# TensorE's instruction order written by the program in a 32-head attention and feed-forward kernel

## The chip, the cores and the metric

The kernel runs on one core of a Trainium2 chip. The time is the device time of one execution in microseconds (us); the figure for a kernel is the median of three runs. A profile is one further execution taken by the hardware profiler; its span runs from the first to the last instruction.

## The reference

The input is 1,024 tokens of 512 numbers, in float32. Attention has 32 heads with 128 numbers for each query, key and value, and is causal. It is followed by a three-layer feed-forward net whose weights are +1 or -1.

```python
x = x + attn(layernorm(x), wq, wkv, wo)
x = x + ffn(layernorm(x), k0, s0, k1, s1, k2, s2)

# attn
q = x @ wq;  k, v = split(x @ wkv)                 # 32 heads of 128
scores = where(causal, q @ k.T * 192 ** -0.5, -1e30)
attn = softmax(scores) @ v
return attn.reshape(S, 32 * 128) @ wo

# ffn
h = relu(s0 * (x @ sign(k0))) * 2
h = relu(s1 * (scaled(h) @ sign(k1))) * 2
return s2 * (scaled(h) @ sign(k2))
```

## The kernel before

**Stages.** The tokens are normalised and transposed into `xnT` (features on the partitions, 1,024 tokens in a row). Queries and keys of the first two heads are computed plainly (`qk_plain`, L256). Then a loop of 256 steps, one for each head and block of 128 queries (L590), does all of attention. The feed-forward net comes last (L724 on).

**Pairs of heads.** Heads go in pairs `g`, 16 steps to a pair; `s` is the step in the pair and `qt` the query block in the head. In the steps of pair `g` TensorE has five kinds of work:

- the scores of the next step's query block, `probabilities` (L448), against all keys up to it, so the work grows with `qt`. The scores have one buffer of two PSUM banks (`ps_sc`, bufs 1), so those of the next step wait until VectorE has read these ones (L458, which also forms `nmax`);
- the products for the pair's values and for the next pair's queries and keys (`products`, L268). Each projection is done by seven half-size products in place of eight (a Strassen-like scheme, with sums of the weights on GpSimd and the combinations on VectorE and ScalarE): 21 products in a pair, in the order values, queries, keys;
- the attention of a head's first 512 queries (the **early attend**, `qb` 0: 4 key blocks) and of its last 512 (the **late attend**, `qb` 1: 8 key blocks), `attend` (L552);
- the products with `wo` for the pair before, 14 parts (`o_products`, L397), which VectorE adds up in `acc`.

**Softmax.** For each step: VectorE adds the mask and finds the row's extreme (L458), ScalarE does the exponential (L469), VectorE the reciprocal (L473), ScalarE the scaling (L474), and VectorE transposes the result in blocks of 32x32 into `tb[qb]` (L480).

**The exchange.** These blocks must still change partitions. `exchange` (L515) does it with DMAs on the SP queue (L524), 16 to a **piece** of four key blocks. A head has three pieces: one for its early attend, two for its late attend. The pieces come from the tile pool `pairs` under the tag `pT`, which has two buffers (L68, L520); a piece can be filled only when the attend that read the buffer before is done with it. `exchange(h, 0)` is written at the step with `qt` 3 and `exchange(h, 1)` at `qt` 7. In the kernel before, the matching `attend` is written four steps later (L620): the early attend at `qt` 7 of its own head, the late one at `qt` 3 of the next.

**What sets the order.** Each engine works through its own instruction stream in order. That stream is made by the tile framework when the program is built: it gives the instructions a priority by their place in the program and puts the first that is ready, by its own model of the times, next on the engine. So an instruction may be put ahead of, or behind, the place where it is written, and one `attend` may be cut in two. The SP queue carries the exchanges and all loads of weights: queries and keys (L122), values (L128) and `wo` (L132).

**The last head** is done differently: its steps run in the order `qt` 4 to 7, 0 to 3, its probabilities are transposed on TensorE (`transpose_last`, L508), and the sums of the `wo` products (`add_products`) and the direct products for the last pair (`o_unit`, L434) fall between its steps.

Of the kernel before, what the change touches and what calls it, by code (L numbers as in the profile page):

```python
# [13 lines left out]
P = 128  # L14
# [15 lines left out]
def kernel(  # L30
# [27 lines left out]
    wq_v = wq.rearrange("(c p) (h e) -> p c h e", p=P, e=DQ)  # L58
    wkv_v = wkv.rearrange("(c p) e -> p c e", p=P)
    wo_v = wo.rearrange("(h p) d -> p h d", p=P)  # L60

    def pool(name, bufs, **kw):
        return ctx.enter_context(tc.tile_pool(name=name, bufs=bufs, **kw))
# [189 lines left out]
        )  # L253
        return dst[h]

    def qk_plain(which, h):  # L256
        dst = new_qk(which, h)
        w = w_raw[which, h // G][:, h % G]
        for half in range(NQB):
            cols = slice(half * QB, (half + 1) * QB)  # L260
            ps = ps_mm.tile([P, QB], F32, tag="mm", name=f"ps_{'qk'[which]}{h}_{half}")
            for c in range(NC):
                nc.tensor.matmul(
                    ps, lhsT=w[:, c, :], rhs=xnT[:, c, cols], start=(c == 0), stop=(c == NC - 1)
                )
            nc.scalar.activation(dst[:, cols], ps, AF.Copy, scale=(-scale, 1.0)[which])

    def products(which, g):  # L268


        s = w_sum[which, g]
        mul = (-scale, 1.0, 1.0)[which]
        n = f"{'qkv'[which]}{g}"
        if which == 2:
            d = []
            for h in (g * G, g * G + 1):
                vs[h] = heads.tile([P, NT, DV], F32, tag="v", name=f"v{h}", bufs=3)
                d.append([vs[h][:, k * TPB : (k + 1) * TPB, :] for k in range(NQB)])
        else:
            d = [  # L280
                [t[:, k * QB : (k + 1) * QB] for k in range(NQB)]
                for t in (new_qk(which, g * G), new_qk(which, g * G + 1))
            ]

        def bank(name):
            shape = [P, TPB, DV] if which == 2 else [P, QB]
            return ps_st.tile(shape, F32, tag="st", name=f"{name}_{n}")

        def kept(name):
            shape = [P, TPB, DV] if which == 2 else [P, QB]  # L290
            return const.tile(shape, F32, tag=name, name=f"{name}_{n}")

        def product(ps, a, b, first, last):
            for c in range(2):
                start, stop = first and c == 0, last and c == 1
                if which != 2:
                    nc.tensor.matmul(  # L297
                        ps,
                        lhsT=a[:, c, :],
                        rhs=b[:, c, :],  # L300
                        start=start,
                        stop=stop,
                        skip_group_check=True,
                    )
                    continue
                for t in range(TPB):
                    nc.tensor.matmul(  # L307
                        ps[:, t, :],
                        lhsT=b[:, c, t * P : (t + 1) * P],
                        rhs=a[:, c, :],  # L310
                        start=start and t == 0,
                        stop=stop and t == TPB - 1,
                        skip_group_check=True,
                    )

        def plus(out, ps, other):
            if which == 0:
                nc.vector.scalar_tensor_tensor(out, ps, mul, other, ALU.mult, ALU.add)
            else:
                nc.vector.tensor_tensor(out, ps, other, ALU.add)  # L320

        X = bank("X")
        product(X, A(which, g, 0, 0), B(0, 0), True, False)
        p1 = kept("p1")
        nc.scalar.activation(p1, X, AF.Copy, scale=mul)  # L325
        yield
        Y = bank("Y")
        product(Y, s[1], T[1], True, False)
        u2 = kept("u2")
        plus(u2, Y, p1)  # L330
        yield
        product(X, A(which, g, 0, 1), B(1, 0), False, True)
        nc.scalar.activation(d[0][0], X, AF.Copy, scale=mul)
        yield
        product(Y, s[2], T[2], False, False)
        u3 = kept("u3")
        plus(u3, Y, p1)
        yield
        Z = bank("Z")
        product(Z, s[0], T[0], True, False)  # L340
        plus(d[1][1], Z, u3)
        yield
        product(Y, A(which, g, 1, 1), T[3], False, True)
        plus(d[1][0], Y, p1)
        yield
        product(Z, s[3], B(1, 1), False, True)
        plus(d[0][1], Z, u2)
        yield
# [25 lines left out]
    def o_products(g):  # L374


        def a(d, i):
            return wo_sb[g][:, i, d * DH : (d + 1) * DH]

        if g not in o_sum:  # L380
            o_sum[g] = sums_of(a, "osum", f"osum{g}", 1)
        s = o_sum[g]
        for m, left, right in (
            (0, lambda: attn[g * G, 0], a(0, 0)),
            (1, lambda: attn[g * G + 1, 0], a(0, 1)),
            (3, lambda: a_sum[g][0], s[0]),
            (2, lambda: a_sum[g][2], s[2]),
            (4, lambda: a_sum[g][1], s[1]),
            (5, lambda: a_sum[g][3], a(1, 1)),
            (6, lambda: attn[g * G + 1, 1], s[3]),  # L390
        ):
            left = left()
            for half in range(2):
                ps = ps_mm.tile([P, 2, DH], F32, tag="mm", name=f"ps_o{g}_{m}_{half}")
                for i in range(2):
                    tok = slice((2 * half + i) * P, (2 * half + i + 1) * P)
                    nc.tensor.matmul(  # L397
                        ps[:, i, :], lhsT=left[:, tok], rhs=right, start=True, stop=True
                    )
                dst = acc[:, m, 2 * half : 2 * half + 2, :]  # L400
                if g == 0:
                    nc.vector.tensor_copy(dst, ps)
                else:
                    nc.vector.tensor_tensor(dst, dst, ps, ALU.add)  # L404
                yield
# [24 lines left out]
    def o_unit(g, t):  # L430
        ps = ps_mm.tile([P, D], F32, tag="mm", name=f"ps_o{g}_{t}")
        k, i = divmod(t, TPB)
        for j in range(G):
            nc.tensor.matmul(  # L434
                ps,
                lhsT=attn[g * G + j, k][:, i * P : (i + 1) * P],
                rhs=wo_sb[g][:, j, :],
                start=(j == 0),
                stop=(j == G - 1),
            )  # L440
        nc.vector.tensor_tensor(xs[t], xs[t], ps, ALU.add)

    def probabilities(h, qt):
        n = (qt + 1) * P
        sc = ps_sc.tile([P, S], F32, tag="sc", name=f"sc{h}_{qt}")
        for first in range(0, n, QB):
            cols = slice(first, min(first + QB, n))
            nc.tensor.matmul(  # L448
                sc[:, cols],
                lhsT=qT[h][:, qt * P : (qt + 1) * P],  # L450
                rhs=kT[h][:, cols],
                start=True,
                stop=True,
            )
# [76 lines left out]
    def attend(h, qb, pieces):  # L531
# [4 lines left out]
        if h == H - 1:  # L536
            ps = ps_mm.tile([P, TPB, P], F32, tag="mm", name=f"ps_av{h}_{qb}")
            for kc in range(nk):
                first = max(0, kc - qb * TPB)
                nc.tensor.matmul(  # L540
                    ps[:, first:, :],
                    lhsT=vs[h][:, kc, :],
                    rhs=last_pT[qb][kc // 2][:, kc % 2, first:, :],
# [5 lines left out]
        ps = ps_mm.tile([P, NB, TPB, B32], F32, tag="mm", name=f"ps_av{h}_{qb}")  # L549
        for kc in range(nk):  # L550
            first = max(0, kc - qb * TPB)
            nc.tensor.matmul(  # L552
                ps[:, :, first:, :],
                lhsT=vs[h][:, kc, :],
                rhs=pieces[kc // TPB][:, kc % TPB, :, first:, :],
                start=(kc == 0),
                stop=(kc == nk - 1),
            )
# [1 line left out]
        if qb == 1 and g + 1 < NG:  # L560
            attn_sums(g, early=(j == 0))

    for which in range(2):
        for h in range(G):
            qk_plain(which, h)
    token_sums()
    weight_sums(2, 0)

# [13 lines left out]
    def softmax_step(h, qt):  # L582
# [3 lines left out]
        else:  # L586
            transpose_last(qt, p)

    softmax_step(*steps[0])
    for i, (h, qt) in enumerate(steps):  # L590
        g, j = divmod(h, G)
        s = i % (G * NT)
        if s == 0:
            chain = products_of_pair(g)
            if g + 1 < NG:
# [17 lines left out]
                load_qk_weights(0, g + 2)  # L613
        if i + 1 < len(steps):
            softmax_step(*steps[i + 1])
        for _ in range(1 + s % 2):
            next(chain, None)
        if qt % TPB == TPB - 1 and h < H - 1:
            qb = qt // TPB
            to_attend[i + TPB] = (h, qb, exchange(h, qb))  # L620
        if i in to_attend:
            attend(*to_attend.pop(i))
        if g > 0 and s >= 2:
            next(o_chain, None)
            if g == NG - 1 and s < 8:
                next(o_chain, None)
        if h == H - 1:
            if qt == 5:
                add_products(x_out)
            if qt == 0:  # L630
                attend(h, 1, None)
# [57 lines left out]
    def hidden_layer(i, k, src, dst):  # L689
        hi, lo = dst  # L690
        for oc in range(NC):
            ps = ffn_bank(f"ps_h{i}_{k}_{oc}")
            for c in range(NC):
                for part in range(2):
                    nc.tensor.matmul(  # L695
                        ps,
                        lhsT=w_sign[i][c][:, oc * P : (oc + 1) * P],
                        rhs=src[part][:, c, :],
# [8 lines left out]
    def output_layer(k):  # L707
        for t in range(k * TPB, (k + 1) * TPB):
            ps = ffn_bank(f"ps_out{t}")
            cols = slice((t % TPB) * P, (t % TPB + 1) * P)  # L710
            for c in range(NC):
                for part in range(2):
                    nc.tensor.matmul(
                        ps,
                        lhsT=h2[k][part][:, c, cols],
                        rhs=w_sign[2][c],
# [60 lines left out]
```

## Time and profile before

| | |
|---|---|
| median of three runs | 1395.57 us (1394.65 to 1396.83) |
| the profiled execution's time | 1395.0 us |
| its span | 1393.2 us |
| TensorE busy | 1358.0 us |
| VectorE busy | 790.8 us |
| ScalarE busy | 491.2 us |
| GpSimd busy | 283.6 us |
| mean granted TensorE clock | 0.997 |

The span is 1.8 us shorter than the execution's time; the rest lies around it. On TensorE a float32 matrix product of one instruction in the program stands as two records in the trace (scores of 512 keys and 128 queries are two records of 128x512). The records' own durations overlap, because matmuls are pipelined; what one costs is read from the distance between starts. "PE" is TensorE's matmul, "DVE" is VectorE, "ACT" ScalarE, "POOL" GpSimd, and "SPq" the queue that issues the DMAs. A row of the waits gives the total, the number and the longest of one kind of wait.

### The profile page before, as it was taken

The numbers are of one execution on the slowest core, as the hardware profiler recorded it, in microseconds if no ns is written. First come the engines' busy times: TensorE is split into PE (matmuls) and PEld (weight loads), VectorE is DVE, ScalarE is ACT, GpSimd is POOL, SyncE is SP. The second block draws the span as 40 slices with busy tenths as digits, with TensorE's granted clock in tenths as the row PEclk, the third lists the DMA queues.
The fourth block names the chain that finished last, engine by engine and source line by source line (L and its number), as shares of the span: only waits on it lengthen the run. The fifth ranks groups of instructions, "written<-read, shape, count | busy, mean of one in ns | idle before, by whom it ended". The sixth has DMA issues, their size and how long they took to land.

```text
span 1393.2 us, 16661 instructions
## 1 busy us (share of the span) xinstructions
PE 1358.0 (97%) x5396; PEld 858.1 (62%) x5396; DVE 790.8 (57%) x1656; ACT 491.2 (35%) x921; POOL 283.6 (20%) x337
## 2 busy tenths in 40 slices
PE   7999999999999999999999999999999999998798
PEld 4647575656657575665757566575756657575467
DVE  3454665555565655556665645565555556656575
ACT  3444343332433333334333323433332343233322
POOL 5211112131111213112121311212131121202400
PEclk9999999999999999999999999999999999999999
DMA  4234434344343434434343443434344343425301
GB/s 151 60 97 104 105 82 123 86 120 104 94 113 83 122 85 125 101 93 119 81 126 83 127 101 91 126 75 127 84 126 102 93 123 77 126 68 143 94 1 61
DMA packets 266421, 139.31 MB, mean 100 GB/s; under 512 B 26208, under 2 KB 259168, under 8 KB 266336
## 3 DMA queue, kind: packets, MB, share of 16 engines
q1 hardware_dynamic: 266336, 138.25, 38.8%
q8 instruction: 44, 0.72, 0.2%
q14 instruction: 41, 0.34, 0.1%
HBM read 38.54 MB, written 2.10 MB: 29 GB/s over the span
## 4 chain that ended last, share of the span: by engine, by line
PE 87%; SPq 5%; DVE 5%; DMA 2%; issue 1%; ACT 0%; POOL 0%; DVEq 0%; ACTq 0%
PE sc L448 16%; PE ps_av L552 15%; PE ps_o L397 11%; PE Y_v L307 6%; PE Y_k L297 5%; PE Y_q L297 5%; SPq L524 5%; PE X_v L307 4%; PE Z_v L307 4%; PE Z_k L297 4%; PE X_q L297 3%; PE X_k L297 3%; PE Z_q L297 3%; PE ps_h L695 2%; DVE tb L480 2%; DMA pT<-tb 1%
## 5 line engine op out<-in xcount | busy, mean ns | idle before, releaser
L469 ACT ACTIVATE p<-p,nmax 128x128 f32<-128x128 f32 (+7 forms) x256 | 197.5, 772 | 396.6 <-DVE nmax L458 395.0
L448 PE MATMUL sc<-kT,qT 128*128 128x512 f32 (+3 forms) x768 | 298.5, 497 | 14.8 <-DVE nmax L458 14.3
L552 PE MATMUL ps_av<-pT,v 128*128 128x512 f32 x744 | 255.4, 486 | 0.0
L458 DVE CUSTOM_DVE_ANT_0 p<-sc,mask 128x128 f32<-128x128 f32 (+7 forms) x256 | 191.3, 747 | 94.1 <-PE sc L448 92.1
L474 ACT ACTIVATE p<-p,rtotal 128x128 f32<-128x128 f32 (+7 forms) x256 | 195.0, 771 | 88.8 <-DVE rtotal L473 88.3
L448 PEld LDWEIGHTS sc<-kT,qT 128*128 128x128 f32 x768 | 136.6, 191 | 142.3 <-issue 82.7
L404 DVE TENSOR_TENSOR acc<-acc,ps_o 128x512 f32<-128x512 f32 x196 | 131.9, 681 | 160.1 <-PE ps_o L397 159.0
L552 PEld LDWEIGHTS ps_av<-pT,v 128*128 128x128 f32 x744 | 140.0, 190 | 129.3 <-issue 107.6
L480 DVE STREAM_TRANSPOSE tb<-p 128x128 f32<-128x128 f32 (+1 forms) x248 | 178.4, 756 | 17.8 <-ACT p L474 14.5
L397 PE MATMUL ps_o<-wo,attn 128*128 128x256 f32 x360 | 87.7, 383 | 0.6 <-POOL attn L369 0.6
L473 DVE RECIPROCAL rtotal<-total 128x1 f32<-128x1 f32 x256 | 39.6, 155 | 74.7 <-ACT p L469 74.3
L397 PEld LDWEIGHTS ps_o<-wo,attn 128*128 128x128 f32 x360 | 67.2, 190 | 20.4 <-issue 8.1
L236 POOL TENSOR_TENSOR wsumq<-wq 128x256 f32<-128x256 f32 x15 | 10.9, 725 | 332.8 <-DMA wq<-in_L_attn_wq_dram 243.7
L307 PEld LDWEIGHTS X_v<-wv,xnT 128*128 128x128 f32 x512 | 63.3, 192 | 4.2 <-issue 0.5
L307 PE MATMUL X_v<-wv,xnT 128*128 128x128 f32 x512 | 65.1, 275 | 0.0
L559 DVE COPY attn<-ps_av 128x512 f32<-128x512 f32 x62 | 41.9, 676 | 37.9 <-PE ps_av L552 37.9
L397 PE MATMUL ps_o<-osum,at 128*128 128x256 f32 x240 | 61.4, 379 | 0.0
L297 PE MATMUL X_q<-xnT,wq 128*128 128x512 f32 x120 | 57.2, 592 | 0.0
L297 PE MATMUL X_k<-xnT,wk 128*128 128x512 f32 x120 | 57.1, 593 | 0.0
L236 POOL TENSOR_TENSOR wsumk<-wk 128x256 f32<-128x256 f32 x15 | 10.9, 725 | 223.7 <-DMA wk<-in_L_attn_wkv_dram 207.3
L397 PEld LDWEIGHTS ps_o<-osum,at 128*128 128x128 f32 x240 | 44.4, 190 | 17.8 <-issue 12.6
L325 ACT ACTIVATE p_k<-X_k 128x512 f32<-128x512 f32 x15 | 8.9, 591 | 114.9 <-PE X_k L297 101.5
(162 smaller groups left out, 1736.0 us busy)
## 6 DMA issues: line engine op xcount, KB each, us to landing
pT<-tb SPq DMA_DIRECT2D x1488, 64.0 KB, 2.0
wq<-in_L_attn_wq_dram SPq DMA_DIRECT2D x32, 256.0 KB, 3.3
wk<-in_L_attn_wkv_dram SPq DMA_DIRECT2D x32, 256.0 KB, 3.4
wv<-in_L_attn_wkv_dram SPq DMA_DIRECT2D x16, 512.0 KB, 4.3
wo<-in_L_attn_wo_dram SPq DMA_DIRECT2D x16, 512.0 KB, 5.0
x_in<-_attn_hidden_states_dram SPq DMA_DIRECT2D x8, 256.0 KB, 5.1
x_out<-_attn_hidden_states_dram SPq DMA_DIRECT2D x8, 256.0 KB, 4.8
out_dram<-osb SPq DMA_DIRECT2D x8, 256.0 KB, 2.0
```

What stands on the lines that cost most here:

```text
L297: nc.tensor.matmul(ps, lhsT=a[:, c, :], rhs=b[:, c, :], start=start, stop=stop, skip_group_check=True,)
L307: nc.tensor.matmul(ps[:, t, :], lhsT=b[:, c, t * P : (t + 1) * P], rhs=a[:, c, :], start=start and t == 0, stop=stop and t == TPB - 1, ski ...
L397: nc.tensor.matmul(ps[:, i, :], lhsT=left[:, tok], rhs=right, start=True, stop=True)
L404: nc.vector.tensor_tensor(dst, dst, ps, ALU.add)
L448: nc.tensor.matmul(sc[:, cols], lhsT=qT[h][:, qt * P : (qt + 1) * P], rhs=kT[h][:, cols], start=True, stop=True,)
L458: nc.vector.tensor_tensor_reduce(out=p[:, :n], in0=sc[:, :n], in1=mask[:, S - n :], scale=1.0, scalar=BIG, op0=ALU.add, op1=ALU.min, accum ...
L469: nc.scalar.activation(p[:, :n], p[:, :n], AF.Exp, bias=nmax, scale=-1.0, accum_out=total)
L474: nc.scalar.activation(p[:, :n], p[:, :n], AF.Copy, scale=rtotal)
L480: nc.vector.transpose(tb[qb][:, : qt + 1, :, i, :], p[:, :n].rearrange("p (c b k) -> p c b k", b=NB, k=B32))
L524: nc.sync.dma_start(pT[b * B32 : (b + 1) * B32, :, a, :, :], tb[qb][a * B32 : (a + 1) * B32, chunks, b, :, :],)
L552: nc.tensor.matmul(ps[:, :, first:, :], lhsT=vs[h][:, kc, :], rhs=pieces[kc // TPB][:, kc % TPB, :, first:, :], start=(kc == 0), stop=(kc ...
L559: nc.vector.tensor_copy(dst.rearrange("p (t a i) -> p a t i", a=NB, i=B32), ps)
```

## The change

1. A wrapper `matmul` keeps an instruction behind everything written for TensorE before it, without waiting for that to finish, while `pinned` is set. It is set for all steps up to the last head's. There TensorE's stream is exactly the program's order.
2. In each step the program now deals out the work by a count of units (one unit is a product of 128x128 with 128x512). A score block has (qt+1)/4 units, an early attend 2.5, a late one 6.5, a projection product 2, a `wo` part 1. A full pair has 92 units, 5.75 for each of its 16 steps. Scores come first in a step; then projection products and `wo` parts are taken until the running count reaches its goal or the quota of each is met; an attend that is due comes behind the first of them, or at the end.
3. The early attend stays four steps behind its exchange; the late one is six behind it, that is at `qt` 5 of the next head.
4. The first queries and keys are computed by halves: the first 512 tokens for all four, then the last 512.
5. In the last pair the `wo` parts are spread over more steps, and `add_products` moves from `qt` 5 to `qt` 7.

```diff
+    def matmul(*args, **kw):
+        ins = nc.tensor.matmul(*args, **kw)
+        if pinned[0]:
+            tc.keep_in_program_order(ins)
...
-    for which in range(2):
-        for h in range(G):
-            qk_plain(which, h)
+    for half in range(NQB):
+        for which in range(2):
+            for h in range(G):
+                qk_plain(which, h, half)
...
+    def score_cols(qt):
+        return (qt + 1) / TPB
+    def value_cols(qb):
+        return qb * TPB + (TPB + 1) / 2
+    PRODUCT, O_PART = 2.0, 1.0
+    ATTEND_AFTER = (TPB, TPB + 2)
     softmax_step(*steps[0])
+    pinned[0] = True
     for i, (h, qt) in enumerate(steps):
...
+        pinned[0] = i + 1 < len(steps) - NT
+        if s == 0:
+            n_chain = 21 if g + 1 < NG else 7
+            n_out = 14 if g > 0 else 0
+            done, chain_done, out_done = 0.0, 0, 0
+            total = (2 * G * sum(score_cols(t) for t in range(NT))
+                + PRODUCT * n_chain + O_PART * n_out)
+            chain_end = 14 if g + 1 < NG else 6
...
         if i + 1 < len(steps):
             softmax_step(*steps[i + 1])
-        for _ in range(1 + s % 2):
-            next(chain, None)
+            done += score_cols(steps[i + 1][1])
         if qt % TPB == TPB - 1 and h < H - 1:
             qb = qt // TPB
-            to_attend[i + TPB] = (h, qb, exchange(h, qb))
-        if i in to_attend:
+            to_attend[i + ATTEND_AFTER[qb]] = (h, qb, exchange(h, qb))
+        late = i not in to_attend
+        if not late:
+            done += value_cols(to_attend[i][1])
+        goal = total * (s + 1) / (G * NT)
+        while True:
+            want_chain = chain_done < min(n_chain, n_chain * (s + 1) / chain_end)
+            want_out = s >= 2 and out_done < min(n_out, n_out * (s - 1) / 14)
+            if want_chain and (done < goal or chain_done + 2 < n_chain * (s + 1) / chain_end):
+                next(chain)
+                chain_done += 1
+                done += PRODUCT
+            elif want_out and (done < goal or out_done + 2 < n_out * (s - 1) / 14):
+                next(o_chain)
+                out_done += 1
+                done += O_PART
+            else:
+                break
+            if not late:
+                attend(*to_attend.pop(i))
+                late = True
+        if not late:
             attend(*to_attend.pop(i))
-        if g > 0 and s >= 2:
-            next(o_chain, None)
-            if g == NG - 1 and s < 8:
-                next(o_chain, None)
         if h == H - 1:
-            if qt == 5:
+            if qt == 7:
+                for _ in o_chain:
+                    out_done += 1
                 add_products(x_out)
```

All other lines of the diff replace `nc.tensor.matmul` by `matmul`, or take the loop over the halves out of `qk_plain`.

More of the change, by code (lines that the diff above doesn't have):

```diff
@@ L60 @@
     wo_v = wo.rearrange("(h p) d -> p h d", p=P)
+    pinned = [False]
+    def matmul(*args, **kw):
+        ins = nc.tensor.matmul(*args, **kw)
+        if pinned[0]:
+            tc.keep_in_program_order(ins)
     def pool(name, bufs, **kw):
@@ L254, in new_qk, with qk_plain @@
         return dst[h]
-    def qk_plain(which, h):
-        dst = new_qk(which, h)
+    def qk_plain(which, h, half):
+        dst = (qT, kT)[which][h] if half else new_qk(which, h)
         w = w_raw[which, h // G][:, h % G]
[L259 to L266, printed above, removed]
+        cols = slice(half * QB, (half + 1) * QB)
+        ps = ps_mm.tile([P, QB], F32, tag="mm", name=f"ps_{'qk'[which]}{h}_{half}")
+        for c in range(NC):
+            matmul(
+                ps, lhsT=w[:, c, :], rhs=xnT[:, c, cols], start=(c == 0), stop=(c == NC - 1)
+            )
+        nc.scalar.activation(dst[:, cols], ps, AF.Copy, scale=(-scale, 1.0)[which])
     def products(which, g):
@@ L296, in product @@
                 if which != 2:
-                    nc.tensor.matmul(
+                    matmul(
                         ps,
@@ L306, in product @@
                 for t in range(TPB):
-                    nc.tensor.matmul(
+                    matmul(
                         ps[:, t, :],
@@ L396, in o_products @@
                     tok = slice((2 * half + i) * P, (2 * half + i + 1) * P)
-                    nc.tensor.matmul(
+                    matmul(
                         ps[:, i, :], lhsT=left[:, tok], rhs=right, start=True, stop=True
@@ L433, in o_unit @@
         for j in range(G):
-            nc.tensor.matmul(
+            matmul(
                 ps,
@@ L447, in probabilities @@
             cols = slice(first, min(first + QB, n))
-            nc.tensor.matmul(
+            matmul(
                 sc[:, cols],
@@ L539, in attend @@
                 first = max(0, kc - qb * TPB)
-                nc.tensor.matmul(
+                matmul(
                     ps[:, first:, :],
@@ L551, in attend @@
             first = max(0, kc - qb * TPB)
-            nc.tensor.matmul(
+            matmul(
                 ps[:, :, first:, :],
@@ L592 @@
         s = i % (G * NT)
+        pinned[0] = i + 1 < len(steps) - NT
[3 more added lines that the diff above has]
+            done, chain_done, out_done = 0.0, 0, 0
+            total = (
+                2 * G * sum(score_cols(t) for t in range(NT))
+                + PRODUCT * n_chain
+                + O_PART * n_out
+            )
+            chain_end = 14 if g + 1 < NG else 6
         if s == 0:
@@ L694, in hidden_layer @@
                 for part in range(2):
-                    nc.tensor.matmul(
+                    matmul(
                         ps,
@@ L712, in output_layer @@
                 for part in range(2):
-                    nc.tensor.matmul(
+                    matmul(
                         ps,
```

## The prediction

> **What bounds the kernel now.** I read the page's first part, then the waits of TensorE, then the timelines of PE and of SP's queue side by side.
>
> ```profile
> span 1393.2 us, 16661 instructions
> ...
> PE 1358.0 (97%) x5396; PEld 858.1 (62%) x5396; DVE 790.8 (57%) x1656; ACT 491.2 (35%) x921; POOL 283.6 (20%) x337
> ...
> pT<-tb SPq DMA_DIRECT2D x1488, 64.0 KB, 2.0
> ```
>
> TensorE is busy for all but 35.2 us, 10 of them before the first products. No order can win more than some 25. The last line is the exchange: 1,488 DMAs, each landing 2.0 us after its issue.
>
> ```profile
> PE sc L448 <- DVE nmax L458: 14.3, 17, 1.8
> PE ptx_a L201 <- DVE xn_a L195: 8.6, 1, 8.6
> ```
>
> So little waits now. How close is the rest to waiting? First PE, then the SP queue (start, duration, what, count):
>
> ```profile
> 617.90 3.60 PE L552 MATMUL ps_av<-pT,v 128*128 128x512 f32 x8
> 621.34 2.94 PE L397 MATMUL ps_o<-wo,attn 128*128 128x256 f32 x12
> ...
> 628.41 2.32 PE L552 MATMUL ps_av<-pT,v 128*128 128x512 f32 x8
> 630.57 1.88 PE L297 MATMUL X_k<-xnT,wk 128*128 128x512 f32 x4
> ...
> 643.93 2.32 PE L552 MATMUL ps_av<-pT,v 128*128 128x512 f32 x8
> ...
> 659.65 3.60 PE L552 MATMUL ps_av<-pT,v 128*128 128x512 f32 x8
> 663.08 1.03 PE L397 MATMUL ps_o<-osum,at 128*128 128x256 f32 x4
> ```
>
> ```profile
> 622.13 10.25 SPq L524 DMA_DIRECT2D pT<-tb  x16
> 632.48 0.54 SPq L128 DMA_DIRECT2D wv<-in_L_attn_wkv_dram  x1
> 633.06 0.54 SPq L132 DMA_DIRECT2D wo<-in_L_attn_wo_dram  x1
> 637.80 21.48 SPq L524 DMA_DIRECT2D pT<-tb  x32
> 659.38 1.11 SPq L122 DMA_DIRECT2D wq<-in_L_attn_wq_dram  x2
> ```
>
> The 16 issues from 622.13 are a head's early piece, the 32 from 637.80 its two late pieces. On PE the late attend is cut in two: its first half (four full key blocks, 3.44 us) at 617.90, its second (2.16) at 628.41, 10 us of other work between; the early attend that needs the piece of 622.13 comes at 643.93. The early piece can't be issued sooner, because both `pT` buffers hold the late pieces of the head before: its issue follows the end of the late attend's first half. It shows again 41 us later: that half ends at 663.08 and the next early piece's issue starts at 663.27. So this chain governs: **first half of late attend, 16 issues, landing, early attend.** Now it takes 643.93-621.34 = 22.6 us of PE's time and needs far less.
>
> What it needs: 0.2 us to the first issue; then 16 issues, at 21.48/32 = 0.67 each, the last one starting after 15x0.67 = 10.1; 2.0 to land; together **12.3 us**.
>
> **The change, part by part.**
>
> *The fixed order.* What one item costs on PE, from distances between starts in the timeline: query and key products 1.72 (626.69 to 628.41), value products 1.79, a `wo` part 0.87, late attend 3.44+2.16, early attend 2.16, scores 0.30 to 1.72 for `qt` 0 to 7. A pair (16 score blocks 15.7, 14x1.72, 7x1.79, 14x0.87, attends 15.5) needs 80.0; now it takes 81.2 (605.00 to 686.23, two heads). I stepped the new loop through a middle pair. The late attend counts 6.5 units where a step's share is 5.75, so the running count passes its goal and the next steps get little. Between the late attend's first half and the early attend stand, in the written order:
>
> - even head (s 5 to 7): second half 2.16, one `wo` part 0.87, scores 1.72, two products 3.44, scores 0.30, one product 1.72: 10.2 us;
> - odd head (s 13 to 15): second half 2.16, scores 1.72, one product 1.72, scores 0.30, one `wo` part 0.87: 6.8 us.
>
> The chain needs 12.3. TensorE must then stand at the early attend: **2.1 us in even heads, 5.5 in odd ones**. Before, other work was drawn into this place; pinned, nothing passes. Queued behind the waiting attend are the next scores, and so the whole softmax chain; nothing makes up for it, since the next late attend comes 27.8 to 28.3 us of PE work later. The late pieces are no problem there: their 32 issues and landing end some 20.5 us after the early attend's start. SP isn't full either (48x0.67 = 32 us of a 44 us head).
>
> Sum: heads 2 to 29 have 14 waits of each kind, 106 us. Head 1 (no `wo` parts yet, one score block and no product at s 14) has 4.2 us of cover and waits 8.1; head 30 (no query or key products left) has 2.16+1.72+1.79+1.08+0.87 = 7.6 and waits 4.7. Together **+119**.
>
> *What it regains.* 1.2 to 1.5 us a pair (81.2 less 80.0; 79.7 with 0.22 for the smallest scores), some 19, and the `nmax` waits of the last pair, some 7 of the 14.3. Between two score blocks there will be at least 1.79 us of other work, against 0.3 to 1.2 for VectorE's reading, so these should go. I take **-24**, bounds -28 and -10.
>
> *The clock.* A wait has a second price:
>
> ```profile
> 1293.67:1297.09 3.42, 2.24 (x6) 1.00 0.40 96
> 1297.09:1300.50 3.41, 1.20 (x7) 1.00 0.43 103
> 1300.50:1303.91 3.41, 1.71 (x4) 0.50 0.44 106
> 1303.91:1307.33 3.42, 3.42 (x13) 0.50 0.29 66
> 1307.33:1310.74 3.41, 2.73 (x10) 1.00 0.40 97
> ...
> 1259.54:1262.95 3.41, 1.77 (x4) 1.00 0.43 103
> ```
>
> (Stretch, length, PE busy, granted clock.) After a stretch of 3.41 us in which PE was 35% busy the clock fell to 0.5, and came back only behind a full one; at 52% it stayed. A wait of 5.5 us leaves some stretch of 3.41 at most 20% busy, so each long wait (15 odd heads and head 30) should drop it. After the wait 1.1 to 4.5 us of work then run at half rate, by where the stretch's edge falls: 0.6 to 2.3 lost, 1.45 in the middle, 16x1.45 = **+23**; bounds 0 and 37. The short waits leave 38% at the worst phase, between the 35% that fell and the 52% that held: 0 to 14x1.45 = 20; by the nearest row they fall, but only in the 38% of phases that put the whole wait into one stretch: **+3**.
>
> The Trainium skill, "TensorE: Matmul & The Clock Gate" (What's actually happening), has the half rate follow at least one idle window of about 3.4 us. The length agrees with the 3.41 here, but the row shows a window 35% busy is enough. By the page only the 61% of long waits that hold a whole window would count, an estimated 14 in place of 23.
>
> *By halves.* The first product starts at 17.05, behind the last transpose, in both orders, and 64 records of 0.43 run to 44.5 either way; PE is never idle in them. **0**, bounds -1 and +1.
>
> *The end.* `add_products` is two steps later (five sums of 2.05 us and two of 1.21 on VectorE) and `wo` parts move into the last head. That head's PE work has room: now early attend of head 30 at 1285.43, second half of its late one at 1319.60, bound by the exchange. **0**, bounds -5 and +8.
>
> Sum on the profiled execution: span 1393.2+119-24+23+3 = 1514, and 1.8 around it (1395.0-1393.2): 1516. The median of the runs, 1395.57, is 0.6 above the profiled one, which changes nothing here.
>
> **Rivals.**
>
> - *The wait without the clock*: the clock holds, as it did at 52%. 1516-26 = **1490**. Against it: the 35% row.
> - *More waits*: the clock falls in the even heads as well (+17), and loads of weights (0.54 to 0.58 an issue, five to seven in a pair) get ahead of early pieces, or `nmax` waits stay: **1546**. For it: `wv` and `wo` are written at s 5 and 6, by the even heads' early piece; against it: they are ready before it.
> - *The early piece isn't held* (other side): if a `pT` buffer were free at its exchange, or the late attend's first half were done 12.3 us of PE work ahead of the early attend, no wait would be left, and only the regained idle: 1395-28 = **1367**, at most no change. It decides at 12.3 us of cover; I count 10.2 and 6.8. Against it: two buffers for three pieces, and 663.08 to 663.27.
> - *The order isn't what is written*, because the framework still moves work into the gap: **1395**. Against it: the pin leaves no freedom.
>
> **How the numbers follow.** The forecast 0.55 (own range 1497 to 1535), clock holds 0.15, more waits 0.17, not held 0.08, order not kept 0.03; the last 0.02 lies between 1400 and 1470. A tenth of the chance lies below the waits; the range of 8 in 10 goes from 1475, the clock's bound, to 1548. What measures as no change here is 0.2% (2.8 us): faster 0.08, same 0.02, slower 0.90.
>
> **What would show it.** TensorE's first wait would be ps_av L552 for DMA pT, some 30 times, long and short in turn, near 119 us in all; the SP queue would wait for ps_av before each early piece; the mean clock would fall to about 0.98, with stretches at 0.50 behind long waits; the pair's period would be near 90. It is wrong if these waits are missing, or if PE's order shows other work between late and early attend.

## The result, and the profile after

The changed kernel takes 1516.80 us (median of six runs, 1515.39 to 1517.19) against 1395.24 for the kernel before, run beside it: a ratio of 1.0869, with a 95% interval of 1.0855 to 1.0883. The profiled execution took 1516.6 us, its span is 1514.8, and its mean clock 0.970.

The changed kernel's page, its time by engines and its chain (shares of the span by engine):

```profile
span 1514.8 us, 16599 instructions
...
PE 1379.9 (91%) x5396; PEld 870.2 (57%) x5396; DVE 815.2 (54%) x1656; ACT 494.2 (33%) x921; POOL 282.4 (19%) x337
...
PE 74%; SPq 17%; DMA 4%; issue 2%; DVE 2%; ACT 0%; DVEq 0%; ACTq 0%
```

TensorE's share of the chain fell from 87% to 74%, and the SP queue's rose from 5% to 17%. TensorE's waits say where (total, number, longest):

```profile
PE ps_av L66 <- DMA pT<-tb: 108.9, 29, 6.5
PE ptx_a L209 <- DVE xn_a L203: 8.7, 1, 8.7
PE ps_pT L515 <- ACT p L481: 5.1, 4, 2.1
PE sc L66 <- DVE nmax L465: 3.8, 4, 1.7
```

The first row was not there before. All products issued through the wrapper now have its line, L66, so the tiles tell them apart. Around one wait of an odd head, TensorE and then the SP queue:

```profile
812.90 5.75 PE L66 MATMUL ps_av<-pT,v 128*128 128x512 f32 x16
818.49 1.88 PE L66 MATMUL sc<-kT,qT 128*128 128x512 f32 x4
820.21 1.88 PE L66 MATMUL Z_k<-xnT,wsumk 128*128 128x512 f32 x4
821.92 0.39 PE L66 MATMUL sc<-kT,qT 128*128 128x128 f32 x2
822.14 1.03 PE L66 MATMUL ps_o<-wo,at 128*128 128x256 f32 x4
828.65 2.69 PE L66 MATMUL ps_av<-pT,v 128*128 128x512 f32 x3 [5.48 <-DMA pT<-tb]
```

```profile
816.52 10.61 SPq L531 DMA_DIRECT2D pT<-tb  x16
```

The queue's own waits (total, number, longest) say what holds the pieces:

```profile
SPq L531 <- PE ps_av L66: 246.0, 30, 12.1
```

The late attend is whole (16 records). Its first half ends at 812.90+3.44 = 816.34, the early piece's first issue follows 0.18 later, and the early attend starts at 828.65, 12.3 us behind that end. Between them TensorE has one score block, one product, the next head's first scores and one `wo` part, and then stands for 5.48 us. The clock in four stretches of this place (stretch, length, PE busy with its records, clock, then the DMA engines' share and GB/s):

```profile
821.22:824.64 3.42, 1.95 (x9) 1.00 0.41 98
824.64:828.05 3.41, 0.00 (x0) 1.00 0.45 107
828.05:831.46 3.41, 2.81 (x4) 0.50 0.37 87
831.46:834.88 3.42, 3.42 (x19) 1.00 0.36 85
```

Behind the idle stretch one stretch runs at half rate. The clock fell at the wait of every odd head, 15 times, for one to three such stretches.

### The profile page after: what moved, and what is told of

Its sections match the earlier page's. It is cut to its first block, busy times and chain, and to the rows that moved or that the text cites. A ratio compares the mean times of both kernels' runs of the same rounds, so it can differ in the third digit from the quotient of the medians.

```text
span 1514.8 us, 16599 instructions
## 1 busy us (share of the span) xinstructions
PE 1379.9 (91%) x5396; PEld 870.2 (57%) x5396; DVE 815.2 (54%) x1656; ACT 494.2 (33%) x921; POOL 282.4 (19%) x337
## 4 chain that ended last, share of the span: by engine, by line
PE 74%; SPq 17%; DMA 4%; issue 2%; DVE 2%; ACT 0%; DVEq 0%; ACTq 0%
SPq L531 17%; PE ps_av L66 14%; PE sc L66 13%; PE ps_o L66 11%; PE Y_v L66 6%; PE Y_k L66 5%; DMA pT<-tb 4%; PE X_v L66 4%; PE Z_v L66 4%; PE Y_q L66 4%; PE X_k L66 3%; PE ps_h L66 2%; PE X_q L66 2%; PE Z_q L66 2%; PE Z_k L66 2%
## 5 line engine op out<-in xcount | busy, mean ns | idle before, releaser
L66 PE MATMUL ps_av<-pT,v 128*128 128x512 f32 x744 | 282.5, 534 | 108.9 <-DMA pT<-tb 108.9
L66 PEld LDWEIGHTS ps_av<-pT,v 128*128 128x128 f32 x744 | 153.0, 210 | 261.2 <-issue 201.6
L66 PE MATMUL sc<-kT,qT 128*128 128x512 f32 (+3 forms) x768 | 291.4, 488 | 3.9 <-DVE nmax L465 3.8
L487 DVE STREAM_TRANSPOSE tb<-p 128x128 f32<-128x128 f32 (+1 forms) x248 | 192.1, 776 | 146.6 <-ACT p L481 86.8
L66 PEld LDWEIGHTS sc<-kT,qT 128*128 128x128 f32 x768 | 140.4, 191 | 92.6 <-issue 76.6
L66 PE MATMUL ps_o<-wo,attn 128*128 128x256 f32 (+1 forms) x392 | 104.3, 397 | 0.8 <-DVE attn L566 0.8
L66 PEld LDWEIGHTS ps_o<-wo,attn 128*128 128x128 f32 x392 | 70.8, 190 | 27.1 <-issue 20.3
L372 POOL TENSOR_TENSOR at<-attn,attn 128x512 f32<-128x512 f32 x15 | 19.0, 1266 | 354.3 <-DVE attn L566 354.3
L66 PEld LDWEIGHTS X_v<-wv,xnT 128*128 128x128 f32 x512 | 62.6, 193 | 5.2
L66 PE MATMUL X_v<-wv,xnT 128*128 128x128 f32 x512 | 62.6, 275 | 0.0
L66 PE MATMUL ps_o<-osum,at 128*128 128x256 f32 x240 | 59.3, 379 | 0.0
L66 PEld LDWEIGHTS ps_o<-osum,at 128*128 128x128 f32 x240 | 45.3, 190 | 23.9 <-issue 20.1
L66 PE MATMUL X_q<-xnT,wq 128*128 128x512 f32 x120 | 56.4, 592 | 0.0
L66 PE MATMUL X_k<-xnT,wk 128*128 128x512 f32 x120 | 56.4, 592 | 0.0
L476 ACT ACTIVATION_READ_ACCUMULATOR p<-p,nmax 128x1 f32 x256 | 47.7, 186 | 0.0
```

The lines of the kernel that those rows point to most:

```text
L66: ins = nc.tensor.matmul(*args, **kw)
L372: nc.gpsimd.tensor_tensor(t0, b(0, 1), b(0, 0), ALU.subtract)
L476: nc.scalar.activation(p[:, :n], p[:, :n], AF.Exp, bias=nmax, scale=-1.0, accum_out=total)
L487: nc.vector.transpose(tb[qb][:, : qt + 1, :, i, :], p[:, :n].rearrange("p (c b k) -> p c b k", b=NB, k=B32))
```

## The experiments

The question was whether the two buffers and the short cover make the loss, or the fixed order itself; and what the clock and each part of the change are worth. Each kernel is compared with runs of the kernel before on the same chip.

**1. A third buffer** (`e1_third_buffer`).

```diff
-    work = pool("work", 3)
+    work = pool("work", 2)
...
-            pT = pairs.tile([P, TPB, NB, TPB, B32], F32, tag="pT", name=f"pT{h}_{qb}_{part}")
+            pT = pairs.tile([P, TPB, NB, TPB, B32], F32, tag="pT", bufs=3, name=f"pT{h}_{qb}_{part}")
```

The two tiles of the feed-forward net that carry the same tag get `bufs=3` as well.

> The changed kernel with three pT buffers in place of two (the room for it comes from the softmax tiles p, of which there are two in place of three). Theory, the early piece is held by the two buffers: with a third one its issue starts at its own exchange, four steps ahead of its attend; all 29 waits for pT (108.9 us) and the clock's falls (some 30 us) go, and the time is 1380 to 1392, a little under the kernel before. Rival, the fixed order is costly whatever the buffers, since TensorE can't pass any late input: the waits move to others (nmax, attn) and the time stays over 1450.

Measured: 1380.38 us, ratio 0.9906 (0.9891 to 0.9921). One wait for `pT` is left, 3.2 us in the first pair. From head 2 to head 28 every pair takes 79.63 us (from an early attend to the one two heads on). So the fixed order alone costs nothing; held pieces do.

**2. The early attend two steps later** (`e2_both_six_late`). Two buffers, as changed.

```diff
-    ATTEND_AFTER = (TPB, TPB + 2)
+    ATTEND_AFTER = (TPB + 2, TPB + 2)
```

> The changed kernel with the early attend six steps behind its exchange as well (two steps, some 10 us of TensorE work, more between late and early attend, so 16 to 20 us of cover for a chain that needs 12.3). Two buffers as before. Theory: no wait for pT is left, the clock stays up, 1380 to 1392. Rival, fixed order costly in itself: over 1450. If the late pieces, which now have four steps in place of six, become late instead, there are waits at the late attend and some 1400 to 1440.

Measured: 1371.73 us, ratio 0.9841 (0.9825 to 0.9857), the fastest place of the attends, and faster than the kernel before. No wait for `pT` is left. TensorE and the SP queue at the same place:

```profile
811.73 5.75 PE L66 MATMUL ps_av<-pT,v 128*128 128x512 f32 x16
...
829.08 1.95 PE L66 MATMUL X_v<-wv,xnT 128*128 128x128 f32 x16
830.87 2.32 PE L66 MATMUL ps_av<-pT,v 128*128 128x512 f32 x8
```

```profile
815.36 24.68 SPq L531 DMA_DIRECT2D pT<-tb  x36
```

The early attend starts 15.7 us behind the end of the late one's first half (811.73+3.44), more than the chain's 12.3, and the row shows no idle time before it.

**3. Nothing pinned** (`e3_not_pinned`).

```diff
-        pinned[0] = i + 1 < len(steps) - NT
+        pinned[0] = False
```

(The line before the loop is set to False too.)

> The changed kernel with nothing kept in program order: the dealing out, the places of the attends and the halves stay. Theory: the framework draws other work between late and early attend as it did before, so no wait for pT is left, 1385 to 1405. Rival, the new places of the attends are the cause and not the pin: still over 1480.

Measured: 1390.83 us, ratio 0.9972 (0.9961 to 0.9983). With the same program text but for the pin, the framework moves other work into the gap: one late attend is cut in two again (halves at 616.27 and 626.58), and the early attend behind it starts at 642.09, 22.4 us after the first half's end. So the loss needs both: the short cover as written, and the pin.

**4. The waits filled** (`e4_filled_waits`).

```diff
         ps = ps_mm.tile([P, NB, TPB, B32], F32, tag="mm", name=f"ps_av{h}_{qb}")
+        for n in range(0 if qb else (5 if h % 2 else 2)):
+            matmul(ps, lhsT=vs[h][:, 0, :], rhs=xnT[:, 2, :QB], start=True, stop=True)
```

> The changed kernel with products that nobody reads put ahead of each early attend, into the same PSUM tile, which the attend then overwrites: five of 0.86 us in odd heads, two in even ones. They stand in the place of the waits (5.3 and 1.9 us), so TensorE's useful work starts when it did. Theory, the falls of the clock cost some 25 to 30 us beside the waits: the clock stays at 1.00 and the time is 1485 to 1495. Rival, the clock costs nothing: 1515 to 1520, unchanged.

Measured: 1486.92 us, ratio 1.0672 (1.0656 to 1.0688), mean clock 0.997. TensorE spends 92 us on products nobody reads (75 and 32 of 0.86) and still waits 19.1 for `pT` (15.7 and, under "issue", 3.4), together 111 in place of 108.9. So the clock alone cost some 30 to 32 us.

**5. The early attend one step later** (`e5_early_five`): `ATTEND_AFTER = (TPB + 1, TPB + 2)`.

> The changed kernel with the early attend five steps behind its exchange, in place of four or six. In the written order the cover between the late attend's first half and the early attend is then 11.5 us in odd heads and 14.0 in even ones (6.7 and 10.1 as changed). Theory, the chain needs 12.0 to 12.3 us and the wait is the difference: waits of 0.5 to 0.8 us in odd heads alone, 7 to 12 us in all, no fall of the clock by them, 1378 to 1386. Rival, the gain of six steps comes from something else that the place of the early attend moves (the softmax chain, buffers): half way between 1372 and 1517, some 1440.

Measured: 1390.12 us, ratio 0.9969 (0.9957 to 0.9981). The waits are what cover and chain leave: 15 of them, all in odd heads, 12.8 us; the first is 2.7, the others 0.4 to 1.3. (The profile puts nine of them, 4.7 us, down to VectorE's `rtotal`; they stand at the same attend.) From head 2 on a pair takes 80.2 to 81.2. The total is 4 us over what was expected, mostly because a wait costs more than its row: from the late attend of head 1 to that of head 29 this kernel takes 1123.77 us (138.51 to 1262.28) and experiment 2 1110.41 (132.57 to 1242.98), so 14 waits whose rows add up to 10.1 cost 13.4, each 0.24 more than its row. Another 4.2 go at head 1, in its wait of 2.7 and a fall of the clock there that experiment 2 doesn't have. From head 28's late attend to the end the two take the same time (159.6 and 159.4).

**6. Both attends four steps behind** (`e6_both_four_late`): `ATTEND_AFTER = (TPB, TPB)`.

> The changed kernel with both attends four steps behind their exchanges, the places of the kernel before, but in the fixed order. The early piece has 16.4 us of cover in odd heads and 19.9 in even ones, so it is not waited for. Theory: the late attend's second half now comes 21.5 to 22 us behind the early attend's start, and its piece is the second of two that go through the queue one after the other once the head's last block is transposed, some 23 to 26 us; so the wait moves there, 1 to 4 us a head, and the time is 1430 to 1480. Rival, the places of the kernel before were right and only the six steps of the late attend did harm: 1370 to 1390.

Measured: 1515.76 us, ratio 1.0866 (1.0848 to 1.0885): as slow as the change, but in another place.

```profile
733.35 2.32 PE L66 MATMUL ps_av<-pT,v 128*128 128x512 f32 x8
751.84 3.60 PE L66 MATMUL ps_av<-pT,v 128*128 128x512 f32 x8
760.38 4.09 PE L66 MATMUL ps_av<-pT,v 128*128 128x512 f32 x8 [4.94 <-DMA pT<-tb]
```

The early attend (733.35) no longer waits; the late one stands 4.94 us between its halves. Waits of 3.3 to 6.7 in one head of a pair and 0.7 to 2.0 in the other make 90 us, 3 a head where 1 to 4 were expected. The total was missed by 36 us: the clock's falls (16, with 92 us at half rate in all) and 18 `nmax` waits (11.2 us) had been left out of it.

**7. Six steps, not pinned** (`e7_six_late_not_pinned`): experiments 2 and 3 together.

> The changed kernel with both attends six steps behind and nothing kept in program order. Tells what the fixed order is worth where nothing waits: the pair took 79.6 us with it and 80.9 to 81.7 without it at four and six steps. Theory, the framework's own order loses some 1 to 1.5 us a pair in short waits: 1385 to 1395. Rival, the places of the attends give the gain and the pin nothing: 1370 to 1375.

Measured: 1394.88 us, ratio 1.0003 (0.9994 to 1.0012). Without the pin the places of the attends move little, and the other way: six steps are 4 us slower than the change's places (1394.88 and 1390.83, the intervals of the ratios apart). From head 2 on a pair takes 80.1 to 82.5 us. The pin is worth 23 us where every transfer is covered, and costs 126 where one isn't (1516.80 against 1390.83).

**8. Without the halves** (`e8_six_late_no_halves`): experiment 2 with the first queries and keys head by head.

> The changed kernel with both attends six steps behind and the first queries and keys in the old order, head by head with both halves of the tokens together. Theory, the order by halves is worth nothing, since TensorE is never idle in these products: within 1.5 us of 1371.7. Rival, by halves the first scores start sooner: 3 to 6 us slower without it.

Measured: 1370.97 us (1369.55 to 1372.55), ratio 0.9830 (0.9816 to 0.9843). The order by halves is worth nothing that can be measured.

**9. The pin alone** (`e9_pin_alone`): the kernel before, its products issued through the wrapper, `pinned` set as in the change.

> The kernel before with nothing changed but the pin: its own program order (one and two products in turn, a wo part a step, both attends four steps behind) kept on TensorE in all steps up to the last head's. Theory, an order written out is only as good as the cover it puts between each issue and its use, and this one puts the late attend's second half too near its piece, as both attends four steps behind did (1515.8): 1490 to 1550. Rival, the pin does no harm to an order that the framework itself starts from: 1380 to 1420.

Measured: 1508.57 us, ratio 1.0823 (1.0799 to 1.0848), with 89.3 us in 16 waits for `pT`; from head 1 on they stand at the second half of a late attend, as in experiment 6, one of 4.9 to 6.3 in each pair. The order that the kernel before is written in is no better when it is kept. What made it fast was that the framework didn't keep it.

**10. Two softmax tiles** (`e10_two_p_tiles`): the control for experiment 1.

> The changed kernel with two softmax tiles p in place of three and nothing else, the control for the third pT buffer, which was paid for with that tile. Theory: the tile is worth nothing while TensorE waits for pT, 1513 to 1523. If it is under 1500, the third buffer's gain was in part that of the smaller pool.

Measured: 1516.98 us, ratio 1.0880 (1.0861 to 1.0898). So the third buffer's gain isn't the smaller pool's.

**11. Only the long waits filled** (`e11_filled_odd_only`): `5 if h % 2 else 0`.

> The changed kernel with five unread products ahead of the early attend in odd heads only, so that the waits of some 1.9 us in even heads stay idle. Tells which waits the clock's loss of 30 us belongs to. Theory, the long ones: the clock still doesn't fall, 1484 to 1492, as with both filled (1486.9). Rival, the short waits carry a share: 1495 to 1510.

Measured: 1496.58 us, ratio 1.0733 (1.0714 to 1.0752): the rival's number. The clock fell behind seven of the short waits, and nowhere at the filled ones. Two stretches that dropped it, with the next, and one that didn't:

```profile
770.81:774.22 3.41, 1.45 (x5) 1.00 0.40 96
774.23:777.64 3.41, 3.41 (x6) 0.50 0.42 101
1122.39:1125.80 3.41, 1.36 (x4) 1.00 0.41 99
1125.80:1129.21 3.41, 3.41 (x8) 0.50 0.41 100
948.31:951.72 3.41, 1.70 (x5) 1.00 0.45 108
951.72:955.13 3.41, 3.41 (x13) 1.00 0.35 82
```

A stretch 40% or 43% busy (1.36 and 1.45 of 3.41) dropped the clock, one 50% busy didn't; in the changed kernel one of 47% (1.61) didn't either (the last section has the other runs). So a wait of 2 us can do it when it falls inside one stretch, and doesn't when an edge divides it. In the changed kernel 13 of the 14 short waits were divided, or left their stretch 47% busy and more; with the long ones filled they stood otherwise to the edges. Seven stretches full of work at half rate lose some 1.7 us each, 12; the waits and the unread products together are 1.3 less than in experiment 4 (109.8 and 111.1). That this makes up the 9.7 us between the two is worked out, not tried.

**12. The pin and six steps, with the old share** (`e12_pin_six_old_share`): experiment 9 with `to_attend[i + TPB + 2]`.

> The kernel before with the pin and with both attends six steps behind, but with its own share of the work: one and two products in turn and one wo part a step, no count of units. Beside the changed kernel with both six steps behind (1371.7) it tells what the even share is worth. Theory, the share matters little once the transfers are covered; a few nmax waits stay where a step holds little work, some 10 us in all: 1378 to 1390. Rival, the even share is what keeps TensorE busy: over 1400.

Measured: 1387.23 us, ratio 0.9950 (0.9933 to 0.9966), with 16.4 us of `nmax` waits, against 4.1 in experiment 2. A full pair takes 80.42 us, against 79.63, so over 15 pairs the even share is worth some 12 of the 15.5 us between 1387.23 and 1371.73. The rest lies outside the full pairs, where the last pair's order differs as well; it wasn't tried apart.

## Why the prediction was right

The mechanism, the place and the total were as forecast: 1516 and 1516.80. The terms were each a little off and the errors cancel, so that the total is right to 1 us is luck.

| term | forecast | measured | from |
|---|---|---|---|
| waits for the early piece | +119 | +115.9 | 108.9 in the rows, and 29 times 0.24 |
| clock | +26 | +30 to +32 | experiment 4 |
| regained | -24 | -24 to -26 | 121.6 (1514.8-1393.2) less the two above |

The 0.24 is what a wait costs beside its row, the same as in experiment 5. An even head whose wait left the clock at 1.00:

```profile
321.57 5.75 PE L66 MATMUL ps_av<-pT,v 128*128 128x512 f32 x16
...
333.39 1.88 PE L66 MATMUL Z_q<-T,wsumq 128*128 128x512 f32 x4
337.00 2.40 PE L66 MATMUL ps_av<-pT,v 128*128 128x512 f32 x8 [1.72 <-DMA pT<-tb]
```

The next late attend starts at 364.82, 43.25 us behind this one, and 41.53 without the wait; in experiment 1, where nothing waits there, the same stretch takes 41.29 (140.43 to 181.72). All 13 even heads without a fall of the clock leave this 0.24 (0.23 in one); for the other waits it is taken over. The row's wait begins at the end of the product's record (333.39+1.88), 0.16 later than the 1.72 that such a product costs in a stream, and the attend's own record is 2.40 in place of 2.32.

- **The chain and the cover.** The chain was put at 12.3; it is 12.0 to 12.5, but for one of 12.7 and one of 13.4 (among its issues is one of 1.57 us). The written order is, item by item, the one that was stepped through. Waits of 2.1 and 5.5 were forecast; they are 1.7 to 2.2 and 5.1 to 5.5, but for one of 3.2, one of 5.9 and head 1's. Head 1's 8.1 became 6.5 and an `nmax` wait of 1.4 inside the same cover.
- **Head 30** was mis-sized: 4.7 forecast, no wait measured. Its early attend lies in step 247, the first that isn't pinned, and the framework put three more of the last head's score blocks, and transposes, before it (the late attend starts at 1388.73, the early one at 1407.19). The diff ends the pin there; the working counted that step as pinned.
- **The clock.** The long waits dropped it every time, as the 35% row had said; their middle cost was 2 rather than 1.45 us (31/16). Of the 14 short ones one dropped it, the longest (3.2 us). The working has the short waits fall in 38% of the phases, which is five falls and some 8 us, but the sum took 3; experiment 11, where seven of 14 fell, shows that the count depends on the edges. The mean clock is 0.970 where 0.98 was forecast. The Trainium skill's rule, at least one idle window ("TensorE: Matmul & The Clock Gate", What's actually happening), would have given an estimated 14 us; seven of the 16 falls here followed a stretch that was 8 to 38% busy, and no stretch of experiment 11 that fell was idle, so here the measurement decides against it.
- **What was regained** was set at 24, and that is what came back. With no wait left, the whole of a pair's loss comes back (79.63 in place of 81.2) and experiment 2 gains 22.8 in all.
- **By halves** and **the end** were put at nothing. Experiment 8 agrees for the first; for the second, 107.8 us lay between head 30's early attend and the end before (1285.43 to 1393.2), and 107.6 now (1407.19 to 1514.8).
- **The rivals.** "The wait without the clock" at 1490 is experiment 4's 1486.92. "Not held" at 1367 is 1380.38 by the third buffer and 1371.73 by the later attend. "More waits" didn't come; SP did carry weight loads ahead of early pieces, and they were through in time. The range's lower end, 1475, is called the clock's bound, but the sum without the clock's term is 1490.

## What to carry to other kernels

Before an order is fixed by hand, work out for each transfer what it needs from the moment its buffer is free (here 12.3 us) and count how much work the written order puts there; a scheduler that may move instructions hides a wrong place, and a pin shows it. Counting TensorE's work into even shares isn't enough: in this kernel one big item (a late attend of 6.5 units) empties the steps behind it, which is just where the cover is needed. When the covers are right, the fixed order wins: two steps' delay of one attend turned a loss of 8.7% into a gain of 1.6%.

## What the runs showed of the hardware

A wait has a second price that its length alone doesn't tell. Cut the changed kernel's profile from 30 us on into stretches of 3.41 us with the edges shown above: each stretch reads a clock of 1.00 or 0.50, none between, and each fall at a wait lasts one to three of them. What goes ahead of a fall is a stretch in which TensorE was less than about half busy. In the profiles of all the runs, from 30 us on, the least busy stretch that kept the clock was 41% busy (1.39 us of 3.41, at 645.30 in experiment 10) and the busiest that dropped it 50% (1.70, at 1318.33 in experiment 1). Between the two both occur: 47% held in the changed kernel (1.61, at 1049.91) and fell in experiment 5 (1.60, at 105.39); what decides there is open. So waits of 2 us dropped the clock once in 14 in the changed kernel, which was its longest, and seven times in 14 in experiment 11, at an estimated 12 us.
